# Additive attention: the exponentials of two query tiles side by side, and one expert part placed in an earlier combination

## The chip, the cores and the metric

The kernel runs on one core of a Trainium2 chip. The metric is the device time in microseconds (us) of one whole execution, the median of three runs. Five engines work side by side, each through its own instructions in their order: TensorE (PE, with its weight loads shown as PEld), VectorE (DVE), ScalarE (ACT), GpSimd (POOL) and SyncE (SP). They wait for one another by semaphores. DMA transfers are started by an instruction on an engine's queue and then run by themselves.

## The reference

`x` is an input of 2 images, 256 channels and 32 x 32 positions, that is 2 x 1024 tokens of 256 numbers. Four layers follow. Layers 0 and 1 are convolution-like attentions, layer 2 is a window attention and a mixture of eight experts, layer 3 an additive attention and another mixture of eight experts. Most of the time goes to layers 0 and 1. What the change touches is the step from layer 2's experts to layer 3:

```python
# layer 2, experts: the two best of eight for each token, weighted
h = gelu(einsum('end,edh->enh', xe, W1) + b1)        # hidden 1024
y = einsum('enh,ehd->end', h, W2) + b2
t = t + (weights[:, :, None] * sel).sum(axis=1)

# layer 3, additive attention; u = layernorm(t), 1024 tokens per image, 32 units
q = u @ Wt;  k = u @ Wx
h = tanh(q[:, :, None, :] + k[:, None, :, :] + bh)   # every query with every key
e = einsum('biju,u->bij', h, Wa[:, 0]) + ba[0]
a = softmax(e, axis=-1)
t = t + einsum('bij,bjd->bid', a, u)

# layer 3, experts: the same idea, hidden 512
```

The additive attention takes a tanh for every query, key and unit: 2 x 1024 x 1024 x 32.

## The kernel before

The program holds two bodies, class `Stack` and class `General`. `General` is for inputs on which the short forms of `Stack` would not be safe. On these inputs `Stack` runs, and all rows of the profile are of it.

**Tiles.** Tokens lie in 16 tiles of 128, eight to an image (`PER` = 8). The additive attention works tile by tile of queries. A tile has eight groups (`FOURS` = 8, `M` in the code), so there are 128 groups, `n` = 0 to 127; image 1 begins at `half` = 64. One group is 16 queries with 32 units each, laid out as four blocks of 128 rows (query and unit) by 1024 keys.

**One group.** `add(n)` (L1282, DVE) adds the query's number to all keys, four blocks of 128x1024, into a buffer `th`; there are three of these. `tangents(n)` (L1292, ACT) takes the tanh of all 128x4096 at once. For the groups that `light` names (n from 50 to 83) ACT adds one block's query itself, as the bias of its tanh (L1289, and L1290 for the other three), and DVE adds three. `score(n)` (L1301, PE) multiplies by `pick`, which sums over units, and collects the scores of a tile in `ps_e`, 128x1024 in PSUM. `ps_e` has one buffer: the next tile's first score waits until the present one has been read.

**One tile's end.** After eight groups `additive_softmax` (L1349) takes the exponential of the scores (L1354, ACT) into `p` and their sum, without a subtraction of the maximum. `turn` (L1314, PE; L1315, DVE) transposes `p` in two halves, `values` (L1322, PE; L1326, DVE) multiplies with the tokens and adds the result to `t`, and `done` takes the tile's statistics for the next norm. The loop says when: tile i's exponential at n = 8 (i + 1), ahead of that step's score, its turns two and three steps later and its values four steps later.

**What runs beside it.** The loop is a generator, and `run` puts other work between its steps (L1584 on). For image 0 this is the rest of layer 2's mixture (`second`): `experts` (L1070) works through 39 blocks of 128 tokens, each in two parts (`up` L1129, `middle` with PE's transposes L1140 and ACT's gelu L1145, `down` L1153), and each `second.step()` brings one part forward. Every second group until n = 49 has a step; at n = 50 what is left is drained. Then `then` combines image 1's experts (`prepare(1, ...)`), whose norm and projection give the keys `kT` (L1253) and queries `qb` that image 1's groups need. From n = 69 (`half + 4`) on, `routed` does layer 3's routing of image 0, and when it is done `first`, layer 3's mixture of image 0 (23 blocks of one part), takes one step at every fourth group. What `first` has left runs in the ending beside the routing of image 1.

**The stage before it.** `prepare(0, ...)` combines image 0's experts. Its first eight steps are one tile each: two loads `yt` from `given` (L1197; one on SP's queue, one on ACT's), two additions to `t` (L1199, DVE) and statistics (L144, L145). Four more steps do the norm and projection (L160, L182, L1248, L1253). In the last four of the twelve, `second` takes a step each.

**Expert weights.** A block's weights come in two transfers on SP's queue, `w1` (L1094) when the block two before has gone through its gelus, and `w2` (L1106). The block's tokens come by a gather on POOL's queue (L1100) and go out by a scatter there (L1160). `turn` of a layer 2 block scales the transposed tokens by numbers that lie in the `w1` tile (L1117, DVE).

**Order.** The order of the source is not the order on an engine. The layer that records the program puts instructions of different steps in an order of its own, by its costs; each engine then keeps that order strictly.

Of the kernel before, what the change touches and what calls it, by code (L numbers as in the profile page):

```python
# [24 lines left out]
F32 = mybir.dt.float32  # L25
# [62 lines left out]
class Stack:  # L88
# [1174 lines left out]
    def additive_attention(self, ctx, aa, t, u, light, done):  # L1263


        tc, nc = self.tc, self.nc
        U, R, J, M = self.UNITS, self.ROWS, self.GROUPS, self.FOURS
        sb = ctx.enter_context(tc.tile_pool(name="aa_sb", bufs=1))
        p_e, p_t = (ctx.enter_context(tc.tile_pool(name=f"aa_{n}", bufs=1, space=PSUM)) for n in "et")
        groups = [(i, m) for i in range(NT) for m in range(M)]  # L1270
        summed, scored = {}, {}

        def keys_and_queries(n, j):
            i, m = groups[n]
            b = i // (N // P)
            return aa["kT"][:, b * N : (b + 1) * N], aa["qb"][:, i, j * M + m : j * M + m + 1]

        def add(n):

            h = sb.tile([P, J, N], F32, name="th", bufs=3)  # L1280
            for j in range(1 if light(n) else 0, J):
                nc.vector.tensor_scalar(h[:, j, :], *keys_and_queries(n, j), None, ALU.add)  # L1282
            summed[n] = h

        def tangents(n):
            h = summed[n]
            if light(n):
                keys, query = keys_and_queries(n, 0)
                nc.scalar.activation(h[:, 0, :], keys, AF.Tanh, bias=query)  # L1289
                nc.scalar.activation(h[:, 1:, :], h[:, 1:, :], AF.Tanh)  # L1290
            else:
                nc.scalar.activation(h, h, AF.Tanh)  # L1292

        def score(n):
            i, m = groups[n]
            if m == 0:
                scored[i] = p_e.tile([P, 2, CH], F32, name="ps_e")
            h = summed.pop(n)
            for a in range(2):
                for j in range(J):  # L1300
                    nc.tensor.matmul(  # L1301
                        scored[i][U * j : U * (j + 1), a, :], lhsT=aa["pick"][:, m, :],
                        rhs=h[:, j, a * CH : (a + 1) * CH], start=(m == 0), stop=(m == M - 1),
                    )
# [12 lines left out]
        def values(i, rec):  # L1317
            b = i // (N // P)
            ptT = turned.pop(i)
            av = p_t.tile([P, 4, P], F32, name="ps_pt").rearrange("p k q -> p (k q)")[:, 0:C]  # L1320
            for j in range(N // P):
                nc.tensor.matmul(  # L1322
                    av, lhsT=ptT[:, j, :], rhs=u[:, b * (N // P) + j, :],
                    start=(j == 0), stop=(j == N // P - 1),
                )
            nc.vector.scalar_tensor_tensor(t[:, i, :], av, rec, t[:, i, :], ALU.mult, ALU.add)  # L1326


        soft = {}
        add(0)  # L1330
        add(1)
        for n in range(len(groups) + 5):
            if n + 2 < len(groups):
                add(n + 2)
            if n < len(groups):
                tangents(n)
            i, m = n // M - 1, n % M
            if i >= 0 and m == 0:
                soft[i] = self.additive_softmax(aa, sb, scored.pop(i))
            if n < len(groups):  # L1340
                score(n)
            if i >= 0 and m in (2, 3):
                turn(i, soft[i][0], m - 2)
            if i >= 0 and m == 4:
                values(i, soft.pop(i)[1])
                done(i)
            yield n

    def additive_softmax(self, aa, sb, pe):  # L1349

        nc = self.nc
        s, rec = (self.small.tile([P, 1], F32, name=f"aa_{n}") for n in ("s", "rec"))
        p = sb.tile([P, N], F32, name="p")
        nc.scalar.activation(p, pe.rearrange("p a b -> p (a b)"), AF.Exp, bias=aa["ba"], accum_out=s)  # L1354
        nc.vector.reciprocal(rec, s)
        return p, rec

# [21 lines left out]
    def run(self):  # L1379
        tc, nc, ins = self.tc, self.nc, self.ins  # L1380
        PER = N // P
        with ExitStack() as ctx:
# [58 lines left out]
            aa = self.additive_weights(ctx.enter_context(tc.tile_pool(name="aa_w", bufs=1)))  # L1441
# [7 lines left out]
            keep = [[enter(ctx, f"keep{layer}{b}") for b in range(B)] for layer in range(2)]  # L1449
# [38 lines left out]
            sb = experts_sb() if self.GUARDED else None  # L1488
# [19 lines left out]
            sb = sb or experts_sb()  # L1508
# [51 lines left out]
            with ExitStack() as side:  # L1560
                bank = in_turn(enter(side, "side_ps", space=PSUM), "m", 3)
                now["bank"] = bank
                ahead.drain()
                weights = ExitStack()
                window.close()
                wp = enter(weights, "ex_w2", bufs=2, side="right")
                other = Steps(ready(0, 1, bank, ahead))
                second = Steps(mixture(
                    0, wp, lambda b: rows[0][0] if b < SURE else all_rows, all_given, BOTH, lambda b: (ahead if b < SURE else other).value
                ))  # L1570
                for k in range(2 * BLOCKS + 3):
                    if k > 1:
                        other.step()
                    if k == 2 * SURE - 5:
                        other.drain()
                        self.extreme(other.value[4][:, 0, 0:1])
                        inv.close()
                    second.step()
                for k, _ in enumerate(prepare(0, bank, enter(side, "outputs2"), PER, nc.sync, nc.scalar)):
                    if k >= PER:  # L1580
                        second.step()


# [1 line left out]
            with ExitStack() as ad:  # L1585
                half = PER * self.FOURS
                bank = banks["h"]
                then = Steps(prepare(1, bank, sb, 3, nc.sync, nc.sync))
                routed = Steps(ready(1, 0, bank))
                first = None  # L1590
                for n in self.additive_attention(
                    ad, aa, t, u, lambda n: half - 14 <= n < half + 20, lambda i: stats(3, i)
                ):
                    if n < half - 2:
                        if n % 2 == 0:
                            second.step()
                        if n > half - 15:
                            second.drain()
                            then.step()
                        if n == half - 3:  # L1600
                            then.drain()
                            weights.close()
                            wp = enter(weights, "ex_w3", bufs=3, side="right")
                    elif n > half + 4 and not routed.done:
                        routed.step()
                    elif routed.done:
                        if first is None:
                            first = Steps(third(0, routed.value))
                        if n % 4 == 0:
                            first.step()  # L1610
# [16 lines left out]
class General(Stack):  # L1627
# [445 lines left out]
                    scores(i + 1)  # L2073
                values(i)

    def additive_softmax(self, aa, sb, pe):
        nc = self.nc
        m, nb, s, rec = (self.small.tile([P, 1], F32, name=f"aa_{n}") for n in ("m", "nb", "s", "rec"))
        nc.vector.tensor_reduce(m, pe, AX.XY, ALU.max)

        nc.vector.tensor_tensor(m, m, aa["ba"], ALU.add)
        nc.vector.scalar_tensor_tensor(nb, m, -1.0, aa["ba"], ALU.mult, ALU.add)
        p = sb.tile([P, N], F32, name="p")
        nc.scalar.activation(p, pe.rearrange("p a b -> p (a b)"), AF.Exp, bias=nb, accum_out=s)
        nc.vector.reciprocal(rec, s)
        return p, rec

# [95 lines left out]
```

## Time and profile before

| what | us |
|---|---|
| median of 3 runs (2513.02 to 2515.34) | 2514.11 |
| the profiled execution's own time | 2513.15 |
| its span | 2511.1 |
| PE busy (94% of the span) | 2357.0 |
| DVE busy (68%) | 1700.8 |
| ACT busy (57%) | 1435.9 |
| first tanh of the additive attention begins | 1748.60 |
| last exponential begins | 2315.1 |

Times in the profile count from the start of the span. A group of instructions is shown by line, engine and operation, with the output and input tiles, then the count, busy time, mean duration in ns, and the idle time of that engine just ahead with what ended it. `ACT_TABLE_LOAD` is ACT changing its function tables; it has the line of the instruction that needed the change. The chain of waits is followed back from the last instruction through what released each. PE's granted clock is 0.977 over the span.

### The profile page before, as it was taken

The numbers are of one execution on the slowest core, as the hardware profiler recorded it, in microseconds if no ns is written. First come the engines' busy times: TensorE is split into PE (matmuls) and PEld (weight loads), VectorE is DVE, ScalarE is ACT, GpSimd is POOL, SyncE is SP. The second block draws the span as 40 slices with busy tenths as digits, with TensorE's granted clock in tenths as the row PEclk, the third lists the DMA queues.
The fourth block names the chain that finished last, engine by engine and source line by source line (L and its number), as shares of the span: only waits on it lengthen the run. The fifth ranks groups of instructions, "written<-read, shape, count | busy, mean of one in ns | idle before, by whom it ended". The sixth has DMA issues, their size and how long they took to land.

```text
span 2511.1 us, 42409 instructions
## 1 busy us (share of the span) xinstructions
PE 2357.0 (94%) x17211; PEld 1029.9 (41%) x17211; DVE 1700.8 (68%) x2616; ACT 1435.9 (57%) x1626; POOL 241.3 (10%) x254
## 2 busy tenths in 40 slices
PE   7999999999999999999998969998999898889987
PEld 4333333333333333333333636664444432334564
DVE  5677777775777777866678566326777788776533
ACT  1565556545555566544453333222999998999222
POOL 0000000000000000000001312221100001111332
PEclk9999999999999999999999989998999999999998
DMA  4000000000000000000000036776334202123897
GB/s 138 1 1 1 1 1 1 1 1 1 1 1 1 1 2 1 1 1 1 1 1 10 2 118 242 295 295 216 129 135 152 76 10 78 66 93 104 290 322 238
DMA packets 58929, 190.51 MB, mean 76 GB/s; under 512 B 14116, under 2 KB 28964, under 8 KB 48740
## 3 DMA queue, kind: packets, MB, share of 16 engines
q1 hardware_dynamic: 45236, 161.86, 18.6%
q0 software_dynamic: 8160, 22.29, 2.5%
q10 hardware_dynamic: 5328, 3.55, 0.5%
q8 instruction: 137, 2.24, 0.4%
q14 instruction: 68, 0.56, 0.1%
HBM read 168.15 MB, written 17.43 MB: 74 GB/s over the span
## 4 chain that ended last, share of the span: by engine, by line
PE 70%; DVE 10%; ACT 8%; issue 7%; DMA 4%; POOL 1%; ACTq 0%; SPq 0%; DVEq 0%; POOLq 0%
PE ps_o L237 20%; PE ps_t L215 19%; PE ps_e L1301 6%; PE bk_h L1129 4%; PE bk_y L1153 4%; ACT th L1292 3%; DVE sum L227 2%; PE ps_row L446 2%; DMA w<-in_l_w 2%; PE ps_pt L1322 2%; PE ps_qk L530 1%; PE ps_row L432 1%; DVE den L263 1%; DVE th L1282 1%; PE ps_row L457 1%
## 5 line engine op out<-in xcount | busy, mean ns | idle before, releaser
L227 DVE TENSOR_TENSOR sum<-sum,e 128x1024 f32<-128x1024 f32 x592 | 725.1, 1225 | 303.7 <-ACT e L218 292.8
L218 ACT ACTIVATE e<-ps_t 128x1024 f32<-128x1024 f32 x640 | 652.8, 1024 | 464.7 <-PE ps_t L216 463.2
L237 PE MATMUL ps_o<-e,v 64*64 64x512 f32 x5120 | 676.6, 592 | 8.5 <-DVE o L244 7.9
L215 PE MATMUL ps_t<-q,k 64*64 64x512 f32 x2048 | 533.9, 592 | 0.5 <-DVE v L571 0.5
L216 PE MATMUL ps_t<-q,k 64*64 64x512 f32 x2048 | 533.8, 592 | 0.0
L1282 DVE TENSOR_SCALAR th<-kT,qb 128x1024 f32<-128x1024 f32 x478 | 331.1, 748 | 92.2 <-PE ps_e L1301 88.0
L237 PEld LDWEIGHTS ps_o<-e,v 64*64 64x64 f32 x5120 | 194.2, 132 | 370.0 <-issue 179.3
L1292 ACT ACTIVATE th<-th 128x4096 f32<-128x4096 f32 x94 | 335.7, 3649 | 5.6 <-DVE th L1282 5.6
L1301 PE MATMUL ps_e<-th,pick 128*32 128x512 f32 x2048 | 273.3, 626 | 25.2 <-ACT p L1354 15.5
L1145 ACT ACTIVATE h<-bk_t,w 128x128 f32<-128x128 f32 x496 | 142.2, 374 | 269.2 <-issue 158.3
L215 PEld LDWEIGHTS ps_t<-q,k 64*64 64x64 f32 x2048 | 149.6, 133 | 287.3 <-issue 153.1
L1129 PE MATMUL bk_h<-w,xgT 128*128 128x512 f32 x496 | 244.6, 610 | 15.5 <-DVE xgT L1117 8.7
L1153 PE MATMUL bk_y<-w,h 128*128 128x256 f32 x992 | 248.6, 387 | 3.0 <-issue 1.0
L1153 PEld LDWEIGHTS bk_y<-w,h 128*128 128x128 f32 x992 | 179.1, 192 | 48.9 <-issue 24.4
L1134 DVE COPY hp<-bk_h 128x512 f32<-128x512 f32 x124 | 85.2, 687 | 131.8 <-PE bk_h L1129 131.7
L265 POOL TENSOR_TENSOR inverses<-inverses,den 128x512 f32<-128x512 f32 x24 | 30.4, 1268 | 1325.9 <-DVE den L263 1325.9
L216 PEld LDWEIGHTS ps_t<-q,k 64*64 64x64 f32 x2048 | 149.4, 133 | 0.0
L215 PE MATMUL ps_t<-qh,kh 64*64 64x512 f32 x512 | 138.3, 598 | 0.0
L216 PE MATMUL ps_t<-qh,kh 64*64 64x512 f32 x512 | 137.5, 596 | 0.0
L1301 PEld LDWEIGHTS ps_e<-th,pick 128*32 128x32 f32 x2048 | 58.8, 112 | 172.1 <-issue 113.6
L1160 POOL DMA_INDIRECT given<-y,gives x85 | 86.6, 1019 | 435.9 <-DVE y L1159 365.6
L1129 PEld LDWEIGHTS bk_h<-w,xgT 128*128 128x128 f32 x496 | 87.5, 193 | 86.8 <-issue 56.1
(334 smaller groups left out, 2057.4 us busy)
## 6 DMA issues: line engine op xcount, KB each, us to landing
w<-in_l_w SPq DMA_DIRECT2D x39, 1152.0 KB, 5.3
w<-in_l_w SPq DMA_DIRECT2D x39, 1030.0 KB, 7.4
w<-in_l_w SPq DMA_DIRECT2D x46, 640.0 KB, 6.2
w<-in_l_w SPq DMA_DIRECT2D x46, 514.0 KB, 4.7
yt<-given SPq DMA_DIRECT2D x40, 128.0 KB, 2.7
rows<-u SPq DMA_DIRECT2D x8, 512.0 KB, 3.7
yt<-given ACTq DMA_DIRECT2D x24, 128.0 KB, 4.2
k<-k SPq DMA_DIRECT2D x16, 128.0 KB, 2.2
```

Source lines behind the costliest of these rows:

```text
L215: nc.tensor.matmul(ps[part, 0, :], lhsT=ka[:, part], rhs=q[0:64, :], start=True, stop=True)
L216: nc.tensor.matmul(ps[part, 1, :], lhsT=kb[:, part], rhs=q[64:128, :], start=True, stop=True)
L218: nc.scalar.activation(e, ps, AF.Exp)
L227: nc.vector.tensor_tensor(c["sum"], c["sum"], e, ALU.add)
L237: nc.tensor.matmul(c["po"][64 * r : 64 * r + 64, half, :], lhsT=v[part, :], rhs=e[part, r, :], start=(j == 0), stop=(j == c["n"] - 1),)
L1129: nc.tensor.matmul(ps, lhsT=inputs[b][:, c, :], rhs=first[b][:, at : at + CH], start=(c == 0), stop=(c == CC - 1),)
L1145: nc.scalar.activation(hidden[b, n][:, cols], ps[:, cols], AF.Gelu, bias=first[b][:, at : at + 1])
L1153: nc.tensor.matmul(sums[b], lhsT=h[:, j * P : (j + 1) * P], rhs=second[b][:, at : at + C], start=(n == 0 and j == 0), stop=(n == HH - 1 an ...
L1160: nc.gpsimd.indirect_dma_start(out=given[b], out_offset=index(slots(b)[1], b), in_=y, in_offset=None)
L1282: nc.vector.tensor_scalar(h[:, j, :], *keys_and_queries(n, j), None, ALU.add)
L1292: nc.scalar.activation(h, h, AF.Tanh)
L1301: nc.tensor.matmul(scored[i][U * j : U * (j + 1), a, :], lhsT=aa["pick"][:, m, :], rhs=h[:, j, a * CH : (a + 1) * CH], start=(m == 0), sto ...
```

## The change

There are three edits in the body that runs.

1. Tiles go in pairs: 0 and 1, 2 and 3, up to 12 and 13; 14 and 15 stay single. When an even tile of a pair is complete, DVE copies its scores from `ps_e` into its buffer `p` (`keep` with `aside`, two copies of 128x512). When the odd tile is complete, a small DVE operation writes `bias`: the last score times zero plus `ba`. Both exponentials take that bias, so neither can begin before the odd tile's scores are there. The even tile's exponential reads and writes `p`, the odd one reads `ps_e`. `p` has two buffers instead of one. The turns and values of the even tile come where those of the odd tile came, and the odd tile's three steps later. The list `due` holds what belongs to which step.
2. In image 0's combination, `second` takes one step more, after the third tile (`k == 2`).
3. The routing of image 0 begins after `half + 6` instead of `half + 4`, since tile 7's values now come at n = 71.

```diff
@@ -1326,7 +1326,45 @@
             nc.vector.scalar_tensor_tensor(t[:, i, :], av, rec, t[:, i, :], ALU.mult, ALU.add)
 
 
-        soft = {}
+
+        soft, due = {}, {}
+        later = lambda n, *fs: due.setdefault(n, []).extend(fs)
+
+        def softmax(*tiles):
+
+
+            bias = self.small.tile([P, 1], F32, name="aa_bias")
+            last = kept[tiles[-1]][1][:, N - 1 : N]
+            nc.vector.scalar_tensor_tensor(bias, last, 0.0, aa["ba"], ALU.mult, ALU.add)
+            for i in tiles:
+                soft[i] = self.additive_softmax(bias, *kept.pop(i))
+
+        def finish(i):
+            values(i, soft.pop(i)[1])
+            done(i)
+
+        kept = {}
+
+        def keep(i, aside):
+
+            p, pe = sb.tile([P, N], F32, name="p", bufs=2), scored.pop(i).rearrange("p a b -> p (a b)")
+            if aside:
+                for a in range(2):
+                    nc.vector.tensor_copy(p[:, a * CH : (a + 1) * CH], pe[:, a * CH : (a + 1) * CH])
+            kept[i] = p, (p if aside else pe)
+
+        for i in range(NT):
+            n = (i + 1) * M
+            aside = i % 2 == 0 and i < NT - 2
+            later(n, lambda i=i, aside=aside: keep(i, aside))
+            if aside:
+                continue
+            tiles = (i,) if i >= NT - 2 else (i - 1, i)
+            later(n, lambda tiles=tiles: softmax(*tiles))
+            for k, tile_of in enumerate(tiles):
+                later(n + 2 + 3 * k, lambda i=tile_of: turn(i, soft[i][0], 0))
+                later(n + 3 + 3 * k, lambda i=tile_of: turn(i, soft[i][0], 1))
+                later(n + 4 + 3 * k, lambda i=tile_of: finish(i))
         add(0)
         add(1)
         for n in range(len(groups) + 5):
@@ -1334,24 +1372,22 @@
                 add(n + 2)
             if n < len(groups):
                 tangents(n)
-            i, m = n // M - 1, n % M
-            if i >= 0 and m == 0:
-                soft[i] = self.additive_softmax(aa, sb, scored.pop(i))
+            todo = due.pop(n, [])
+            if n % M == 0:
+
+                while todo:
+                    todo.pop(0)()
             if n < len(groups):
                 score(n)
-            if i >= 0 and m in (2, 3):
-                turn(i, soft[i][0], m - 2)
-            if i >= 0 and m == 4:
-                values(i, soft.pop(i)[1])
-                done(i)
+            for f in todo:
+                f()
             yield n
 
-    def additive_softmax(self, aa, sb, pe):
+    def additive_softmax(self, ba, p, pe):
 
         nc = self.nc
         s, rec = (self.small.tile([P, 1], F32, name=f"aa_{n}") for n in ("s", "rec"))
-        p = sb.tile([P, N], F32, name="p")
-        nc.scalar.activation(p, pe.rearrange("p a b -> p (a b)"), AF.Exp, bias=aa["ba"], accum_out=s)
+        nc.scalar.activation(p, pe, AF.Exp, bias=ba, accum_out=s)
         nc.vector.reciprocal(rec, s)
         return p, rec
 
@@ -1577,7 +1613,8 @@
                         inv.close()
                     second.step()
                 for k, _ in enumerate(prepare(0, bank, enter(side, "outputs2"), PER, nc.sync, nc.scalar)):
-                    if k >= PER:
+
+                    if k == 2 or k >= PER:
                         second.step()
 
 
@@ -1601,7 +1638,7 @@
                             then.drain()
                             weights.close()
                             wp = enter(weights, "ex_w3", bufs=3, side="right")
-                    elif n > half + 4 and not routed.done:
+                    elif n > half + 6 and not routed.done:
                         routed.step()
                     elif routed.done:
                         if first is None:
...
```

Left out is the same change of `additive_softmax`'s arguments in `General`, which does not run here.

More of the change, by code (lines that the diff above doesn't have):

```diff
@@ L2074, in window_attention, with additive_softmax @@
                 values(i)
-    def additive_softmax(self, aa, sb, pe):
+    def additive_softmax(self, ba, p, pe):
         nc = self.nc
         m, nb, s, rec = (self.small.tile([P, 1], F32, name=f"aa_{n}") for n in ("m", "nb", "s", "rec"))
[L2079 to L2084, printed above, removed]
+        nc.vector.tensor_reduce(m, pe, AX.X, ALU.max)
+        nc.vector.tensor_tensor(m, m, ba, ALU.add)
+        nc.vector.scalar_tensor_tensor(nb, m, -1.0, ba, ALU.mult, ALU.add)
+        nc.scalar.activation(p, pe, AF.Exp, bias=nb, accum_out=s)
         nc.vector.reciprocal(rec, s)
```

## The prediction

> **What bounds the kernel now.** I read the page first (engines in 40 slices, then its costliest groups), next ACT's groups over the additive attention (1746.5 to 2318 us of the span), then the stage table, and last the timeline around one exponential and in the combination before.
>
> ```profile
> PE   7999999999999999999998969998999898889987
> ...
> DVE  5677777775777777866678566326777788776533
> ACT  1565556545555566544453333222999998999222
> ...
> L1282 DVE TENSOR_SCALAR th<-kT,qb 128x1024 f32<-128x1024 f32 x478 | 331.1, 748 | 92.2 <-PE ps_e L1301 88.0
> ...
> L1134 DVE COPY hp<-bk_h 128x512 f32<-128x512 f32 x124 | 85.2, 687 | 131.8 <-PE bk_h L1129 131.7
> ```
>
> A slice is 62.8 us. In slices 28 to 36 ACT stands at nine tenths or more, nowhere else. That is the additive attention. Its groups on ACT:
>
> ```profile
> L1292 ACT ACTIVATE th<-th 128x4096 f32<-128x4096 f32 x94 | 335.7, 3649 | 5.6 <-DVE th L1282 5.6
> ...
> L1145 ACT ACTIVATE h<-bk_t,w 128x128 f32<-128x128 f32 x158 | 45.6, 388 | 11.2 <-PE bk_t L1140 11.1
> ...
> L1354 ACT ACTIVATE p<-ps_e,sb_ba 128x1024 f32<-128x1024 f32 x16 | 17.8, 1112 | 2.0 <-PE ps_e L1301 1.8
> L1354 ACT ACT_TABLE_LOAD x12 | 15.4, 1283 | 0.2
> L1145 ACT ACT_TABLE_LOAD x12 | 15.4, 1283 | 0.2
> ```
>
> Tanh (L1292) has no table load of its own; the exponential (L1354) and the experts' gelu (L1145) have 12 each, so one exponential among gelus costs two loads. In order of time (start, duration, instruction):
>
> ```profile
> 1784.41 1.28 ACT L1354 ACT_TABLE_LOAD   x1
> 1785.71 1.11 ACT L1354 ACTIVATE p<-ps_e,sb_ba 128x1024 f32<-128x1024 f32 x1
> 1786.72 0.19 ACT L1354 ACTIVATION_READ_ACCUMULATOR p<-ps_e,sb_ba 128x1 f32 x1
> 1786.93 1.28 ACT L1145 ACT_TABLE_LOAD   x1
> 1788.22 1.14 ACT L1145 ACTIVATE h<-bk_t,w 128x128 f32<-128x128 f32 x4
> ```
>
> The next such load begins at 1821.14 and the sixth at 1968.94: (1968.94 - 1784.41) / 5 = 36.9 us for a tile of eight groups. Busy time of PE, PEld, DVE, ACT, POOL by stage (us), then granted clock and DMA:
>
> ```profile
> 1746.50:1969.00 222.50, 219.65 (x1314) 104.82 (x1313) 176.36 (x294) 217.52 (x170) 23.45 (x21) 1.00 0.40 136
> 1988.00:2040.00 52.00, 44.49 (x258) 17.30 (x260) 44.22 (x132) 48.46 (x30) 0.97 (x1) 0.93 0.15 44
> 2147.00:2318.00 171.00, 153.93 (x956) 65.79 (x955) 129.01 (x227) 169.69 (x108) 23.80 (x21) 0.96 0.26 89
> 2318.00:2376.00 58.00, 54.58 (x260) 36.46 (x258) 36.12 (x126) 17.94 (x53) 18.87 (x20) 1.00 0.82 276
> 1714.90:1746.50 31.60, 19.51 (x64) 11.12 (x63) 23.93 (x86) 3.76 (x11) 1.96 (x2) 0.78 0.51 179
> ```
>
> ACT binds both expert stretches (98% and 99%); PE stands close behind in the first (99% busy, as its ends are modelled). In the combination (last row) PE has 12 us free.
>
> **The change, part by part.** Counts are from the order in which the built program of the changed kernel stands on each engine.
>
> *Table loads.* Seven pairs and two single tiles give 9 exponential events for 16. Loads fall from 12 + 12 to 8 + 8: 8 x 1.283 = 10.3 us of ACT. Six of them go before the score of group 51, two after 2147. All lie where ACT binds.
>
> The Trainium skill (ScalarE: Activation LUTs, What ACT_TABLE_LOAD costs) gives a switch as a 1283 ns load and a drain of about 1380 ns, 2.66 us; 8 of those would be an estimated 21.3 us. In the row above the exponential begins 0.02 us after the load ends and the load right after the tanh, so no drain is seen and the load alone is counted.
>
> *Expert parts moved.* After the first tanh of image 0, ACT has 25 groups of four gelus where it had 27; before the last exponential of image 1, 9 where it had 11. A group adds 1.00 us (1752.13 to the next tanh at 1753.13): 4.0 us. ACT relief is 14.3 us in all: 7.7 + 2.0 in image 0, 2.6 + 2.0 in image 1.
>
> *How much PE lets through.* By the chain of waits, PE gives a score of one group 1.85 us (8 per tile: 14.8), a part 1.72 up, 0.44 transposes, 1.73 down and some 0.1 (4 per tile: 16.0), a tile's turns and values 0.9 + 3.45. That is 35.1 of 36.9 us. ACT needs 98% of 36.9, 36.2, and with 9.7 / 6 = 1.6 us less per tile 34.6: PE would then be the longer of the two. The gain lies between none and all; I take nine tenths in image 0 (six tiles by 36.9 - 35.1 = 1.8 us would be 10.8, so there is room for 9.7, but hardly for waits): 8.7 of 9.7 us; 4.1 of 4.6 in image 1, where PE has 17 us free.
>
> *Copies.* Seven tiles get two 128x512 copies from PSUM: 14 x 0.687 = 9.6 us of DVE, 1.4 per tile. Beside the experts DVE is 79% and 75% busy, so they hide under tanhs (3.65 against 2.74 us of adds per group). If the adds behind them come late, each costs up to 1.4. Tile 6's copies fall into image 1's combination (1988 to 2040), where DVE is 85% busy and ACT afterwards waits 2.0 us for keys (kT): bounds 0 to 1.4, I take 1.4. The two of tiles 8 and 10 lie around the routing, where ACT already waits for adds up to 2.5 us: 0 to 2.8, I take 1.0.
>
> The Trainium skill (VectorE: DVE Perf Modes, Rules for kernel authors) advises copying PSUM to SBUF first only where many operations follow; one does here. By that rule the copies are a loss of 9.6 us; the ACT saving behind it is what the rule doesn't count.
>
> *Bias operation and waits.* Nine 128x1 operations, near the reciprocal's 0.16 us: 1.5 us of DVE. Each waits for its score, as the adds beside it do. Nothing is added for them.
>
> *Tile 6's exponential* (1.11 and its load 1.28, at 2006.44) lay before the wait for kT, which hid it. It now comes with tile 7's behind that wait: 0 to 2.4 us, I take 2.4, for ACT is busy from there on.
>
> *The part in image 0's combination (k == 2).* Its matrix work fits this wait of PE:
>
> ```profile
> 1722.89 1.12 PE L1140 MATMUL bk_t<-ident,hp 128*128 128x128 f32 x4 [7.45 <-ACT h L1145]
> ```
>
> Its gather and scatter go to POOL, busy 2.0 of 31.6 us here, and cost nothing. ACT's eight yt loads now have eight gelus between them where they had one; the loads come at 0.6 us each and the gelus have their input early, so I add nothing for that. But on SP its 1.03 MB w1 fetch goes in after three of eight yt loads, before the other five. On DVE the scaling xgT of its input, which waits for that fetch, stands after six of the 16 combining operations. In the trace a fetch issued at 1722.28 served an xgT at 1728.22, at most 5.9 us; issued near 1717 it lands by 1723, where DVE in the trace had gone one tile (1.2 us) further. Later in the queue, y waits for PE's four up and down matmuls behind the second xgT (about 2). Bounds -1 (PE work taken away in front) and +6; I take 3.6 for the first tanh.
>
> *The routing two groups later* (half + 6). One layer 3 part fewer is done by the last group. In the built order it stands in the ending after the dispatch, in front of the transposes that wait for gathered tokens: PE goes empty there from 2365.9 to 2373.3, most of it on one line of the chain of waits:
>
> ```profile
> 2368.52 4.62 DMA xg<-rows,takes
> ```
>
> A part takes 4.0 us of PE and fits; its 1.15 MB takes 4.2 us at 276 GB/s. Bounds 0 and 4, I take 1.0.
>
> Sum: -8.7 - 4.1 + 1.4 + 1.0 + 2.4 + 3.6 + 1.0 = -3.4. The last image-0 part is also drained about one light group earlier in the built order (3.7 us, bounds 0 and 3.7; I take 2.7): -6.1. The profiled execution took 2513.15 (span 2511.1 and 2.05 around it), 0.96 under the median 2514.11, so 2513.15 - 6.1 + 0.96 = 2508.0.
>
> **Rivals.**
> - *The pair holds the score bank too long (slower).* ps_e has one buffer. From the end of the old exponential's tanh it was held about 2.4 us; now another tanh and two exponentials stand in between: 3.65 + 1.28 + 2.4 = 7.3. The built order puts 6.4 us of expert matmuls there at the first pair, but only 3.3 at image 1's. A stall counts beyond the 3.8 us that two tiles have free; if PE idles 4.9 us at the six pairs with experts, the pairs first give back the gain of 12.8 (-6.1 + 12.8 = +6.7, 2521), and 1.1 x 6 = 6.6 more when all six do (2527). It decides from about half of the gain lost, 6 us. For: single waits of 4.29 and 3.36 us on p. Against: those lie in the stretch without experts.
> - *PE takes over in image 0 (no change).* None of the 8.7 comes: +2.6, and 2514 to 2517. For: 219.65 of 222.5. Against: 1.8 us per tile that the sum of its work leaves.
> - *All relief arrives, costs hide:* -14.3, 2500. For: PE's 12 free us in the combination; against: the DVE queue there.
> - *Nothing is done*, if scheduling split the pairs: excluded, each pair's exponentials stand next to each other on ACT.
>
> **How the numbers follow.** 0.2% is 5.0 us, about what a measurement of this kernel can tell. The forecast, with its own range of 2503 to 2512, has 0.45 (0.36 of it below 2509.1); full relief 0.15; PE-bound 0.17 (0.12 within); the held bank 0.23. Faster 0.51, same 0.21, slower 0.28. Range 2499 to 2523: full relief below, the held bank's lower price above.
>
> **What would show it.** 16 loads in the attention; tile period in image 0 near 35.5 us; first tanh near 1752; kT's wait on ACT longer than 2.0; the last exponential 5 to 7 us earlier; the gap before the gathered tokens filled. PE waiting for p over 3.8 us per pair, or a first tanh past 1755, would prove me wrong.

## The result: 0.36% slower

The changed kernel took 2524.29 us in the median of 7 runs (2516.85 to 2527.25), the kernel before 2515.34 (2513.02 to 2519.37): ratio 1.0036, 95% interval 1.0022 to 1.0050. The forecast was 2508.0 in a range of 2499 to 2523. The profiled execution of the changed kernel is its fastest one (2516.85, span 2515.0), so the profile shows less of the loss than the median.

From the page of the changed kernel, the engines in 40 slices, and the two groups whose idle time (after the second bar) answers those shown before:

```profile
PE   7999999999999999999998979998999887889996
...
DVE  5677777775777777775678656327787767786543
ACT  1566556545655565543554333224999988998221
...
L1282 DVE TENSOR_SCALAR th<-kT,qb 128x1024 f32<-128x1024 f32 x478 | 330.2, 750 | 71.7 <-PE ps_e L1301 68.6
L1292 ACT ACTIVATE th<-th 128x4096 f32<-128x4096 f32 x94 | 336.6, 3641 | 13.5 <-DVE th L1282 13.3
```

ACT now stands at eight tenths in three of the slices 28 to 36, where it had one. The tanhs of L1292 wait 13.3 us for their adds where they waited 5.6. The loads went as the order had said; ACT's groups over the additive attention of the changed kernel:

```profile
L1390 ACT ACT_TABLE_LOAD x8 | 10.3, 1283 | 0.1
L1145 ACT ACT_TABLE_LOAD x8 | 10.3, 1283 | 0.1
```

To compare executions that start the attention at different moments, I count from the first tanh to the last exponential. Busy time of PE, PEld, DVE, ACT, POOL, then granted clock and DMA: the kernel before, from tile 5's exponential to tile 11's, and over the whole stretch:

```profile
1970.23:2180.14 209.91, 181.75 (x1093) 70.44 (x1091) 166.76 (x395) 196.16 (x125) 18.45 (x17) 0.95 0.15 51
...
1748.60:2315.09 566.49, 522.23 (x3154) 225.77 (x3153) 442.88 (x862) 547.69 (x373) 59.49 (x53) 0.97 0.28 94
```

and the changed kernel:

```profile
1961.71:2182.49 220.78, 179.36 (x1074) 68.49 (x1074) 169.26 (x399) 195.75 (x123) 15.60 (x15) 0.92 0.14 47
...
1742.95:2314.47 571.52, 507.20 (x3108) 221.74 (x3108) 447.89 (x879) 535.05 (x355) 54.33 (x49) 0.96 0.26 87
```

ACT has 547.7 - 535.1 = 12.6 us less to do, near the 14.3 forecast. Its idle time, the length less ACT's busy time, went from 566.5 - 547.7 = 18.8 to 571.5 - 535.1 = 36.5, by 17.7. The stretch is 5.0 us longer, and the middle alone 10.9 longer (the exponentials of a pair stand one tanh later in the queue than the old ones, so single marks are good to some 3.7 us; the whole stretch has no such error). The relief came; waits ate more than all of it. What ACT waited for there, in the kernel before:

```profile
ACT th L1292 <- DVE th L1282: 5.6, 7, 2.5
...
ACT uT L184 <- PE bk_h L182: 4.3, 4, 1.8
ACT th L1289 <- DVE kT L1253: 2.0, 1, 2.0
...
ACT rt_flat L879 <- PE bk_h L874: 0.5, 1, 0.5
```

and in the changed kernel (us in total, times, longest):

```profile
ACT th L1292 <- DVE th L1282: 13.3, 14, 2.1
ACT p L1390 <- DVE aa_bias L1338: 4.7, 2, 3.6
ACT uT L184 <- PE bk_h L182: 4.6, 3, 3.6
ACT th L1289 <- PE ps_e L1301: 3.8, 2, 2.4
ACT th L1289 <- DVE kT L1253: 3.6, 1, 3.6
ACT th L1290 <- DVE th L1282: 2.2, 2, 1.9
ACT rt_flat L879 <- PE bk_h L874: 1.9, 1, 1.9
```

No single wait makes the loss. PE's timeline shows where they begin, in the light groups around image 1's combination and layer 3's routing:

```profile
2000.69 8.72 PE L1301 MATMUL ps_e<-th,pick 128*32 128x512 f32 x50 [4.48 <-DVE p L1353]
...
2040.25 1.11 PE L1314 MATMUL ps_pt<-ident,p 128*128 128x128 f32 x4 [8.27 <-ACT p L1390]
...
2110.74 1.12 PE L1314 MATMUL ps_pt<-ident,p 128*128 128x128 f32 x4 [6.87 <-ACT p L1390]
```

At tile 6 the score bank is released by the copy on DVE (PE waits 4.48 us), and the scores of three groups then stand in one block. At the pairs (6,7) and (8,9) PE stands 8.27 and 6.87 us for p with later scores behind it; beside the experts this wait is at most 2.65. PE's clock is lower in this part as well: 0.92 between the exponentials of tiles 5 and 11, where the kernel before has 0.95 (the third number from the end of the rows above).

### The profile page after: what moved, and what is told of

It is laid out like the page before. It is cut to its first block, busy times and chain, and to the rows that moved or that the text cites. A ratio compares the mean times of both kernels' runs of the same rounds, so it can differ in the third digit from the quotient of the medians.

```text
span 2515.0 us, 42454 instructions
## 1 busy us (share of the span) xinstructions
PE 2351.8 (94%) x17211; PEld 1031.3 (41%) x17211; DVE 1708.8 (68%) x2639; ACT 1425.9 (57%) x1618; POOL 240.1 (10%) x254
## 4 chain that ended last, share of the span: by engine, by line
PE 69%; DVE 11%; ACT 8%; issue 6%; DMA 4%; POOL 1%; ACTq 0%; DVEq 0%; SPq 0%; POOLq 0%
PE ps_o L237 20%; PE ps_t L215 19%; PE ps_e L1301 5%; PE bk_h L1129 4%; ACT th L1292 4%; PE bk_y L1153 4%; DMA w<-in_l_w 3%; DVE sum L227 2%; PE ps_row L446 2%; PE ps_pt L1322 2%; DVE th L1282 2%; PE ps_qk L530 1%; PE ps_row L432 1%; DVE den L263 1%; PE ps_row L457 1%
## 5 line engine op out<-in xcount | busy, mean ns | idle before, releaser
L1292 ACT ACTIVATE th<-th 128x4096 f32<-128x4096 f32 x94 | 336.6, 3641 | 13.5 <-DVE th L1282 13.3
L1301 PE MATMUL ps_e<-th,pick 128*32 128x512 f32 x2048 | 266.6, 621 | 22.4 <-ACT th L1292 12.0
```

The source lines that it names most:

```text
L1301: nc.tensor.matmul(scored[i][U * j : U * (j + 1), a, :], lhsT=aa["pick"][:, m, :], rhs=h[:, j, a * CH : (a + 1) * CH], start=(m == 0), sto ...
```

## The experiments

Every run is compared with the kernel before on the same chip. "Stretch" is first tanh to last exponential in the run's one profiled execution, "idle" is ACT's part of it without work. All runs but k2_alone and half6_alone keep the changed kernel's loop and the two buffers of `p`; tied3, which adds three bias operations to that, is as fast as the kernel before, so this frame costs nothing that can be told.

| Run | Ratio, 95% interval | Stretch | ACT idle |
|---|---|---|---|
| before | 1 | 566.5 | 18.8 |
| changed kernel | 1.0036 (1.0022 to 1.0050) | 571.5 | 36.5 |
| again | 1.0034 (1.0021 to 1.0048) | 575.9 | 40.4 |
| k2_alone | 1.0010 (0.9997 to 1.0023) | 566.2 | 20.2 |
| half6_alone | 0.9997 (0.9982 to 1.0011) | 565.6 | 19.0 |
| pairs_half6 | 1.0021 (1.0008 to 1.0034) | 573.9 | 37.0 |
| sparse | 0.9975 (0.9964 to 0.9986) | 562.1 | 24.8 |
| sparse_again | 0.9972 (0.9960 to 0.9983) | 560.6 | 23.6 |
| undo_light | 0.9988 (0.9977 to 0.9999) | 559.8 | 25.6 |
| image0 | 0.9993 (0.9983 to 1.0003) | 563.4 | 23.6 |
| sparse2 | 0.9987 (0.9976 to 0.9999) | 561.6 | 27.1 |
| early | 0.9983 (0.9972 to 0.9994) | 561.3 | 25.9 |
| light | 1.0042 (1.0027 to 1.0056) | 577.3 | 29.7 |
| copies | 1.0027 (1.0016 to 1.0038) | 575.3 | 24.3 |
| copies3 | 1.0044 (1.0031 to 1.0057) | 579.2 | 28.1 |
| tied | 1.0020 (1.0006 to 1.0035) | 572.0 | 21.3 |
| tied3 | 0.9995 (0.9983 to 1.0007) | 566.8 | 19.1 |
| late | 1.0019 (1.0006 to 1.0031) | 567.9 | 21.3 |

### The three parts of the change

**again** is the changed kernel unaltered.

> The changed kernel itself once more. Its one profiled execution took 2516.85 us, its other six 2521.3 to 2527.3, so some 8 us of the loss have no profile yet. Theory A (the rest is in the ending, where the waits for weights and gathered tokens vary): a profile of 2521 or more has its last exponential near 2314.5 as before, and the added microseconds after it. Rival B (it is in the attention): the last exponential comes 4 us or more later than 2314.5. Ratio to the kernel before 1.003 to 1.005.

Measured: 2522.36 (2519.65 to 2525.85), profiled 2525.85. Theory A fell: the last exponential came late, as rival B has it, though most of that was lost before the attention. The ending took 196.3 us, as in the kernel before (196.0). The last exponential came 13.3 us later than in the first profile: 8.95 us by the first tanh, 5.1 of them already before the projection (L432) that begins at 548 us, and 4.4 more in the stretch. So single executions of one program differ by that much (see the last section), and the stretch is the steadier measure.

**k2_alone**:

```diff
-                    if k >= PER:
+                    if k == 2 or k >= PER:
                         second.step()
```

> Kernel before with the k == 2 part only. The profile of the changed kernel has its first tanh near 1743 where the kernel before has 1748.6: theory A, the part alone did that (-5.6 us, where my forecast said +3.6), and the lead is carried through: 4 to 6 us faster, ratio 0.998. Rival B: the lead came from the pairs or is given back at the routing, as in the changed kernel: less than 2 us faster.

Measured: 1.0010, first tanh at 1748.63. Theory A fell. The early first tanh of the changed kernel (1742.95) came from an execution whose self-attention ended 4.7 us sooner, not from this part. The part seems to cost: 2.5 us by this ratio (0.0010 x 2514), 3.3 where it is added to the pairs (1.0034 against 1.0021); k2_alone's interval reaches no change, and the intervals of the other two overlap. The profiles agree with it: from the first addition of image 0's combination (L1199) to the first tanh it is 31.3 us in the kernel before and 30.0 to 32.5 in the thirteen others without the part, but 33.4 to 34.6 in the four profiles with it. In k2_alone the combination also began 3.1 us earlier, so its first tanh did not move.

**half6_alone**:

```diff
-                    elif n > half + 4 and not routed.done:
+                    elif n > half + 6 and not routed.done:
                         routed.step()
```

> Kernel before with the routing two groups later only. The ending of the changed kernel holds 36 groups of gelus where the kernel before holds 35, and took 200.5 us from the last exponential where it took 196.0. Theory A: one layer 3 part more in the ending costs its whole 4.5 us: +4 to +5 us, ratio 1.0018. Rival B (the forecast's term): it fills the gap before the gathered tokens, +1.0 us, within the noise.

Measured: 0.9997, so rival B: one part more in the ending cannot be told from nothing. The endings of all profiles (last exponential to the end) lie between 195.5 and 201.7 us, with the part and without it. The pairs need this step: the first step of the routing reads what tile 7 leaves, and a pair leaves it three groups later.

**pairs_half6** takes the `k == 2` part out of the changed kernel:

```diff
-                    if k == 2 or k >= PER:
+                    if k >= PER:
                         second.step()
```

> Changed kernel without the k == 2 part. Theory A (the pairs lose by themselves, most of it where no gelus lie between the exponentials, and the k == 2 part wins some 5 us): about 5 us slower than the changed kernel, ratio to the kernel before 1.005 to 1.007. Rival B (the pairs win in image 0 and the k == 2 part costs): as fast as the kernel before or faster, ratio 1.000 or less.

Measured: 1.0021, stretch 573.9, idle 37.0, between the two bounds. The pairs (with the later routing) lose by themselves, as theory A has it; that the `k == 2` part would win was wrong.

### Which pairs

**light** keeps three pairs of the seven, **sparse** the other four, both without the `k == 2` part and light with the later routing (exponentials that stand alone have neither copy nor bias operation):

```diff
-            aside = i % 2 == 0 and i < NT - 2
+            aside = i in (6, 8, 10)          # sparse: (0, 2, 4, 12)
...
-            tiles = (i,) if i >= NT - 2 else (i - 1, i)
+            tiles = (i - 1, i) if i - 1 in (6, 8, 10) else (i,)   # sparse: (0, 2, 4, 12)
```

> Kernel before with the pairs (6,7), (8,9) and (10,11) only, with their copies and bias operations, and the routing two groups later, which these pairs need (its first step reads what tile 7 leaves). At most one exponential load goes. Theory A: first tanh to last exponential 571 to 575 us, with ACT idle near 3.5 us before the pair (8,9) as in the changed kernel; ratio 1.002 to 1.003. Rival B (these pairs only make room for idle time that was there before): 568 us or less, ratio 1.001 or less.

> Kernel before with pairs only where they save table loads: tiles (0,1), (2,3), (4,5) and (12,13); the other exponentials single, at their old places, without a bias operation; routing and combination as before. It saves the same 8 loads, 10.3 us of ACT. Theory A (the loss of the changed kernel sits in the pairs (6,7), (8,9), (10,11), which save no load): from the first tanh to the last exponential 561 to 564 us (before 566.5, changed kernel 571.5), ratio 0.997 to 0.9995. Rival B (ACT's relief comes back as idle time wherever it is won, since keys, adds or PE set the pace): 566 us or more, ratio 1.000 or above.

Measured: light 1.0042, sparse 0.9975 (2507.63 against 2513.57). This is the result of the study: theory A in both, with light's stretch of 577.3 above its bounds. Light, ACT's loads in the attention and the stretch (middle, whole):

```profile
L1392 ACT ACT_TABLE_LOAD x12 | 15.4, 1283 | 0.2
L1145 ACT ACT_TABLE_LOAD x12 | 15.4, 1283 | 0.2
```

```profile
1965.02:2189.72 224.70, 178.38 (x1067) 68.08 (x1065) 168.34 (x397) 200.32 (x125) 16.60 (x16) 0.92 0.14 47
...
1743.36:2320.61 577.25, 516.70 (x3136) 225.13 (x3135) 445.70 (x868) 547.53 (x369) 56.28 (x51) 0.96 0.26 90
```

These three pairs save no load at all: 12 and 12, as before, because no gelu stands between the exponentials of tiles 6 to 10, and the pair (10,11) only moves tile 10's behind the first gelus of layer 3, where tile 11 needs its load anyway. ACT's work is the same (547.5 for 547.7), and its idle time is 10.9 us longer. The four other pairs save all eight loads; here is their repetition:

**sparse_again**

> The kernel with the four loading pairs (0,1), (2,3), (4,5), (12,13) once more, since its ratio of 0.9975 stands beside 0.9987 for a kernel with one pair more and a first-tanh-to-last-exponential span that differs by half a microsecond. Theory A (it is really the fastest, 5 us or more under the kernel before): 0.997 to 0.9985. Rival B (the two differ by the ending of single executions only): 0.9985 or more.

Measured: 0.9972 (2506.11 against 2514.02). Its loads, and its stretch:

```profile
L1392 ACT ACT_TABLE_LOAD x8 | 10.3, 1283 | 0.1
L1145 ACT ACT_TABLE_LOAD x8 | 10.3, 1283 | 0.1
```

```profile
1963.46:2174.09 210.63, 183.62 (x1112) 72.36 (x1112) 168.64 (x400) 192.51 (x125) 19.38 (x17) 0.96 0.15 50
...
1746.00:2306.60 560.60, 516.17 (x3156) 225.93 (x3155) 446.75 (x874) 537.01 (x365) 66.35 (x54) 0.98 0.27 95
```

ACT's work is 10.7 us shorter, idle time 4.8 longer, the stretch 5.9 shorter. Theory A holds twice. This version, 0.28% under the kernel before, beats both kernels.

**undo_light** takes the pairs (6,7), (8,9), (10,11) apart in the changed kernel and leaves the rest of the change:

```diff
-            aside = i % 2 == 0 and i < NT - 2
+            aside = i in (0, 2, 4, 12)
...
-            tiles = (i,) if i >= NT - 2 else (i - 1, i)
+            tiles = (i - 1, i) if i - 1 in (0, 2, 4, 12) else (i,)
```

> Changed kernel with the pairs (6,7), (8,9), (10,11) taken apart, and nothing else undone: the combination's part and the later routing stay; exponentials that stand alone are without copy and without bias operation. Theory A (these three pairs are the loss): first tanh to last exponential near 562 us, as with the four loading pairs alone, and the ratio 0.997 to 1.000. Rival B (the loss needs the combination's part or the later routing together with pairs): 566 us or more, ratio above 1.001.

Measured: 0.9988, stretch 559.8. Undoing three pairs turns 1.0034 into 0.9988. Against sparse it has the `k == 2` part and the later routing more, and seems 3 to 4 us slower (the intervals touch), near the price of that part again; its stretch is no longer than sparse's.

### What such a pair costs

> Kernel before with the two copies of each of the seven tiles 0, 2, .. 12 out of PSUM, each exponential alone and at its old place, reading the copy; no pair, no bias operation. 14 copies of 0.69 us are 9.6 us of DVE, and the exponential now waits for them. Theory A (the copies hide under the tanhs beside the experts): first tanh to last exponential within 2 us of 566.5. Rival B (they are what holds the pairs back): 3 us or more longer, ratio 1.001 to 1.003.

> Kernel before with the bias operation on DVE for each of the 16 exponentials, no copies and no pairs: the exponential waits not for its score but for a DVE operation that waits for the score and stands in DVE's queue. In the changed kernel the pair (8,9) waited 3.55 us for that operation. Theory A (the wait costs where DVE has the routing in its queue, 2 to 4 us): first tanh to last exponential 568 to 571 us. Rival B (forecast: nothing): within 1 us of 566.5.

```diff
 both (all singles; tied has the bias operation for each, copies has none):
-            aside = i % 2 == 0 and i < NT - 2
+            aside = i in ()
-            tiles = (i,) if i >= NT - 2 else (i - 1, i)
+            tiles = (i - 1, i) if i - 1 in () else (i,)
 copies besides:
-            later(n, lambda i=i, aside=aside: keep(i, aside))
+            later(n, lambda i=i: keep(i, i in (0, 2, 4, 6, 8, 10, 12)))
```

Measured: copies 1.0027 and tied 1.0020; both do harm alone: rival B for the copies, and for the bias operation theory A's size, but not its place. Each also has one load more of each kind than before (13 and 13), since one group of gelus moved between exponentials, and 3.3 and 3.0 us more ACT work by that. Tied's idle time is 2.5 us longer; it grew ahead of image 1's keys (7.7 us between tile 5 and the keys, 4.6 before) and not in the routing, where theory A looked for it (9.6 from the keys to tile 11, 9.2 before). To find which part hurts on the tiles of the light pairs, three further runs do one part each there:

**copies3**: `keep(i, i in (6, 8, 10))`, all singles. **tied3**: `if tiles[-1] in (7, 9, 11):` ahead of the bias operation. **late**, with the later routing:

```diff
+                at = n + {6: M, 8: M, 10: M, 7: 3, 9: 3, 11: 3}.get(i, 0)
-                later(n + 2 + 3 * k, lambda i=tile_of: turn(i, soft[i][0], 0))
+                later(at + 2 + 3 * k, lambda i=tile_of: turn(i, soft[i][0], 0))
```

(and likewise for the second turn and the values.)

> Kernel before with the two copies for tiles 6, 8 and 10 only, each exponential alone at its old place and reading the copy; no bias operation, routing as before. With the three pairs of these tiles, first tanh to last exponential went from 566.5 to 577.3 us, all of it ACT idle time (18.8 to 29.7). Theory A (the loss is the copies' place in DVE's queue, before the keys and in the routing): 571 us or more, idle 24 or more. Rival B (it is the bias operation's wait) and rival C (it is the later turns and values): 566 to 568.

> Kernel before with the bias operation for the exponentials of tiles 7, 9 and 11 only; no copies, no pairs, routing as before. Rival B (the wait on DVE's queue is the loss): 570 us or more between first tanh and last exponential, with 2.5 to 3.5 us of ACT idle before tile 9's exponential. Theory A and rival C: 566 to 568.

> Kernel before with only the later places that the pairs give to the turns and values of tiles 6 to 11 (those of 6, 8, 10 eight groups later, those of 7, 9, 11 three later), and the routing two groups later; exponentials single and at their old places, no copies, no bias operations. Rival C (values late, so the layer norm, the routing and their transposes late): 570 us or more, with waits of 3 us or more for the layer norm's transposes and the routing near tile 8. Theory A and rival B: 566 to 568, as with the later routing alone (565.6).

Measured: copies3 1.0044 with idle 28.1, tied3 0.9995 with 19.1, late 1.0019 with 21.3. Theory A: by the ratio six copies of 0.69 us are enough for the whole loss of light (1.0042), by idle time for 9.2 of its 10.9 us. Copies3, middle and whole, and PE at tile 6:

```profile
1966.00:2188.23 222.23, 186.64 (x1093) 70.99 (x1091) 169.83 (x399) 199.53 (x127) 18.50 (x17) 0.93 0.15 48
...
1744.34:2323.57 579.23, 524.96 (x3154) 226.85 (x3153) 447.23 (x868) 551.18 (x376) 59.63 (x53) 0.96 0.27 92
```

```profile
2006.84 7.27 PE L1301 MATMUL ps_e<-th,pick 128*32 128x512 f32 x48 [6.36 <-DVE p L1355]
```

The kernel before, same place:

```profile
2008.99 7.13 PE L1301 MATMUL ps_e<-th,pick 128*32 128x512 f32 x34 [4.29 <-ACT p L1354]
```

DVE has 447.2 - 442.9 = 4.3 us more to do, and the stretch is 12.7 longer: 3.5 of ACT work (most of it one more load of each kind) and 9.2 of idle. At tile 6 the copy stands in DVE's queue behind the combining operations and adds; the bank comes free 2.1 us later after the first tanh (262.5 against 260.4), 48 score matmuls stand in a block instead of 34, and the keys come 4.2 us later. How the rest of those 4.2, and the 8.2 between the keys and tile 11 (3.1 of them ACT work), divide among the queues I can't separate. Late's stretch agrees with theory A (+1.4 us), but its ratio is clear of 1; its ending was 201.6 us, within the scatter of endings, so part of its 1.0019 stays unplaced, and the later turns and values are not cleared.

How far the waits of light come from its copies is open, for the three kernels lose in different places (us; the windows are from tile 5's exponential to the keys, and from the keys to tile 11's exponential):

| Run | Keys after the first tanh | ACT idle to the keys | ACT idle, keys to tile 11 | Clock, keys to tile 11 |
|---|---|---|---|---|
| before | 290.9 | 4.6 | 9.2 | 0.95 |
| light | 291.9 | 7.7 | 16.6 | 0.90 |
| copies3 | 295.1 | 8.5 | 14.2 | 0.92 |
| copies | 296.9 | 8.5 | 9.9 | 0.96 |

The rows from the keys to tile 11, in the same order:

```profile
2039.49:2180.14 140.65, 120.08 (x748) 44.09 (x740) 113.80 (x249) 131.50 (x76) 16.51 (x15) 0.95 0.17 58
2035.27:2189.72 154.45, 118.99 (x736) 45.72 (x728) 116.25 (x255) 137.81 (x79) 14.66 (x14) 0.90 0.16 53
2039.42:2188.23 148.81, 124.08 (x748) 44.90 (x740) 115.54 (x251) 134.59 (x78) 16.55 (x15) 0.92 0.16 55
2040.76:2185.05 144.29, 119.19 (x748) 43.68 (x740) 115.65 (x251) 134.36 (x77) 16.49 (x15) 0.96 0.17 57
```

Up to the keys ACT idles 3 to 4 us more in all three, which have tile 6's copies in common. Behind the keys the run copies, which has these same six copies and eight more, idles 0.7 us more than the kernel before and copies3 5.0, so what copies3 loses there is not a fixed price of a copy. Light idles most there, and it has what copies3 lacks: PE waits 8.27 us at tile 7, where copies3 and the kernel before have 3.36, for PE's next work there is the transposes of tile 6, whose exponential now comes only with tile 7's. The clock is lower where the waits are longer. Whether that makes them longer still, and how much the pair itself adds to its copies, no run separates: pairs without copies need a second score bank and were not tried.

### How much of the relief can be had

**image0**, on the kernel before:

```diff
+            aside = i in (0, 2, 4)
...
+            tiles = (i - 1, i) if i - 1 in (0, 2, 4) else (i,)
```

> Kernel before with the pairs (0,1), (2,3), (4,5) only. 6 of the 8 loads go, 7.7 us of ACT. Theory A (image 1's keys end image 0's stretch, so that most of the relief comes back as ACT's wait for them): keys about 2 us earlier after the first tanh (288.8 against 290.9), ACT idle 9 us or more between tile 5's exponential and the keys, first tanh to last exponential 563 to 565. Rival B (the gain is won here): 560 to 562. Ratio 0.998 to 1.000.

Measured: 0.9993, stretch 563.4, keys 288.8 after the first tanh, ACT idle 10.2 us between tile 5 and the keys (4.6 before). Theory A: of 7.7 us relief some 3 arrive. Up to tile 5's exponential ACT is idle 4.0 us (3.8 before), so the relief comes that far and is lost behind it. In image0, sparse and sparse2 ACT waits 6 us for the keys (3.0 in undo_light); sparse_again:

```profile
2034.76 2.19 ACT L1289 ACTIVATE th<-kT,qb 128x1024 f32<-128x1024 f32 x2 [6.02 <-DVE kT L1253]
```

**sparse2** has (11,12) and (13,14) in place of (12,13); **early** adds to it the light groups, the drain and the combination two groups earlier:

```diff
+            aside = i in (0, 2, 4, 11, 13)
...
-                    ad, aa, t, u, lambda n: half - 14 <= n < half + 20, lambda i: stats(3, i)
+                    ad, aa, t, u, lambda n: half - 16 <= n < half + 20, lambda i: stats(3, i)
...
-                        if n > half - 15:
+                        if n > half - 17:
```

> As the kernel with the four loading pairs, but in image 1 the pairs (11,12) and (13,14) in place of (12,13): one exponential load and one gelu load more go, 10 in all. Theory A (ACT sets the pace from tile 11 on): 2.6 us less than the 562.1 between first tanh and last exponential, ratio 0.996 to 0.998. Rival B (the second pair's relief becomes idle time there): 562 or more.

> The kernel with the pairs (0,1), (2,3), (4,5), (11,12), (13,14) and image 1's combination, with its light groups and the drain of layer 2's parts in front of it, two groups earlier. In the kernel with loading pairs ACT waits 6.0 us for the keys. Theory A (the combination's chain sets when the keys come): the wait shrinks below 3 us and first tanh to last exponential drops by another 3 to 5 us against the kernel without this step, ratio 0.994 to 0.997. Rival B (PE, with the expert parts crowded in front, sets it): no gain.

Measured: sparse2 0.9987, early 0.9983: neither is under sparse, though the wait for the keys was gone in early (what it has there is 2.81 us for scores). ACT's work in sparse2 is 534.5 us, 2.5 under sparse_again, and its idle time 3.5 over it. Rival B in both, with sparse2's stretch of 561.6 just under its bound: taking the wait for the keys away did not bring the relief back.

## Why the prediction was wrong

- *Table loads and ACT relief* (14.3): right. 8 and 8 loads in the attention, 12.6 us less ACT work. The load alone counts, as the rows said: sparse drops 8 loads and ACT's work falls by 10.4 to 10.7 us, against 10.3 for the loads. The Trainium skill's figure (ScalarE: Activation LUTs, What ACT_TABLE_LOAD costs), with its drain an estimated 21.3, is not seen here.
- *The cost of the light pairs* (copies 1.4 + 1.0, tile 6's exponential 2.4, bias operations nothing, 4.8 in all): the step that failed. These three pairs cost 10.8 us of the stretch (light), and undoing them turns 1.0034 into 0.9988, 11.6 us. The term most mis-sized is the copies: copies on the same three tiles alone made the stretch 12.7 us longer, 9.2 of it ACT waiting. I priced a copy at its own duration ("bounds 0 to 1.4" and "0 to 2.8"). At tile 6 it stands in DVE's queue behind the combination and takes over from ACT the release of the only score bank; in copies3 a block of scores, the layer norm and the keys are late then. The working even had DVE at 85% there, and took the 1.4 as the most that could come. How the loss behind the keys divides between copies, held bank and clock is open. The Trainium skill's rule that I weighed and set aside (VectorE: DVE Perf Modes, Rules for kernel authors: copy out of PSUM first only for many operations) points the right way. The copies' own time is 9.6 us for seven tiles; copies alone made the stretch 8.8 longer, 3.3 of them ACT work.
- *Bias operations* (nothing): on the three light tiles alone right (tied3, idle 0.3 us longer); in the changed kernel ACT waited 4.7 us for them.
- *Who saves what*: I summed loads and costs over seven pairs. Pair by pair it would have shown that four save eight loads and three save none: no exponential of tiles 7 to 10 has a load of its own in the kernel before. The working never set a pair's saving against its cost.
- *Through PE* (8.7 in image 0, 4.1 in image 1): too much. Image 0's three pairs bring 3 of 7.7. The step that let it down is not PE's sum, which passes the relief up to tile 5, but what stands behind: ACT waits 10.2 us between tile 5 and the keys where it waited 4.6, and early shows that the keys are not the only late input there. The four pairs bring 4.4 and 5.9 us of the stretch in their two profiles, 6 to 8 by the medians. In image 1 the pair (12,13) brings 0.5 to 2.5 us of 2.6 (tile 11 to tile 15: 134.5 and 132.5 in the two runs of sparse, 135.0 in image0).
- *Tile 6's exponential behind the keys* (2.4): load and exponential now stand between the keys and tile 7, as forecast; it is a cost of a light pair, not measured by itself.
- *The k == 2 part* (3.6): near, in size and in place: 2.5 by the ratio alone, 3.3 in the changed kernel, and a combination that is some 3 us longer in the profiles, though no interval of these ratios excludes a price of nothing.
- *Routing two groups later* (1.0): not contradicted, -0.8 with an interval of 3.6 to either side. I read PE as empty from 2365.9 to 2373.3; it has 4.8 us of work there and only 2.6 without, so the term had less room than I thought. *Earlier drain* (-2.7): not seen by itself.
- *The rival of the held bank* had the right time, 2521 to 2527, and I gave it 0.23. I argued against it that the long waits "lie in the stretch without experts", which is where two of the pairs are and a third begins. My own sign for it, PE waiting for p over 3.8 us, came there: 8.27 and 6.87. That its time fits is in part luck: it took the loss from six pairs beside experts, where no more than five stand, and the four of them that save loads win.

Taken together: forecast -6.1 us, measured +9.0. The light pairs cost some 6 us more than I had for them, the relief that arrives is 5 to 7 less than the 12.8, and the 2.7 of the drain did not show; by these runs that is the 15 us between the two, within the noise.

## What to carry to other kernels

Price a batching change unit by unit: each pair must show the load that it saves, and one that saves none has only costs. An operation that moves onto a nearly full engine can cost more than its duration (here 4.1 us of copies and a stretch 12.7 longer), above all if it becomes the one that frees a single buffer. When the engine that binds is relieved, look for the next late input (here the second image's keys, and when they came earlier the scores), for the relief stops there.

## What was not expected of the hardware

One program's executions differ early on. The first profile of the changed kernel, busy time by stage with the granted clock third from the end:

```profile
500.00:530.00 30.00, 30.00 (x248) 10.18 (x244) 24.45 (x22) 15.96 (x18) 1.27 (x1) 1.00 0.00 1
530.00:550.00 20.00, 18.87 (x152) 7.74 (x148) 16.87 (x35) 8.65 (x10) 0.00 (x0) 1.00 0.00 1
```

and the second (again):

```profile
500.00:530.00 30.00, 30.00 (x252) 10.16 (x244) 24.00 (x21) 16.40 (x18) 1.27 (x1) 1.00 0.00 1
530.00:550.00 20.00, 18.87 (x121) 7.89 (x120) 15.55 (x35) 6.15 (x6) 0.00 (x0) 0.83 0.00 1
```

At the same idle gap of 1.13 us of PE, the clock fell in one execution and not in the other: (1 - 0.83) x 20 = 3.4 us of PE lost there. The next projection (L432) starts at 548.1 instead of 543.0; the gap itself came 1.7 us later. With such differences the kernel before alone ran from 2505.8 to 2523.7 us over 29 runs, and a first tanh that is 5.6 us earlier proved nothing about the edit in front of it.
